# Attention's copies out of PSUM, issued half a slot later, on one core of Trainium2

## The chip, the core and the metric

The kernel runs on one core of one Trainium2 chip. A core has a matrix engine (TensorE, PE in the profile, with its weight loads shown apart as PEld), a vector engine (VectorE, DVE), an activation engine (ScalarE, ACT), GpSimd (POOL) and a queue that issues DMAs (SyncE, SP). Each engine has its own stream of instructions, and semaphores tie the streams together. The metric is the device time of one launch in microseconds (us), the median of several runs; lower is better.

## What is computed

The input x is 4 x 32 x 96 x 256 (batch, variables, segments, channels). Layer 0 normalizes it by groups of channels and sends it through two selective-scan blocks (Mamba), one along the segments and one along the variables. Layer 1 takes the 3072 tokens of each batch, normalizes them, adds attention and then a mixture of four experts, whose gate comes from a graph attention over about a million edges. The part that matters here is the attention, an additive one in which every pair of tokens passes a tanh over 32 units:

```python
def _L1_attn_ref(inputs, Wt, Wx, bh, Wa, ba):
    q = jnp.einsum('bld,du->blu', inputs, Wt)
    k = jnp.einsum('bld,du->blu', inputs, Wx)
    h = jnp.tanh(q[:, :, None, :] + k[:, None, :, :] + bh)
    e = jnp.einsum('biju,u->bij', h, Wa[:, 0]) + ba[0]
    a = jax.nn.softmax(e, axis=-1)
    v = jnp.einsum('bij,bjd->bid', a, inputs)
    return v
...
    x = x + _L0_conv_ref(_gn(x), ...)
    t = _to_tokens(x)
    t = t + _L1_attn_ref(_ln_t(t), L1_attn_Wt, L1_attn_Wx, L1_attn_bh, L1_attn_Wa, L1_attn_ba)
    t = t + _L1_ffn_ref(_ln_t(t), ...)
```

## The kernel before

**Two streams of work, interleaved by hand.** The order of PE, ACT, DVE and POOL is exactly the order in which the program issues instructions; no scheduler moves them. In `whole`, one generator, `att.units`, issues attention, and at each of its `yield`s another one, `steps`, issues a piece of the other work: first layer 0 (`Layer0.run`), then the sorting of edges and a part of the experts. One step of `units` is a *slot*. A slot has two halves:

- attention issues one `th` (L802: a tanh over 128 x 3072 on ACT, for 4 query tokens and 32 units); then comes the first half of the other work;
- attention issues the scores of the `th` of two slots ago (L778, on PE, into the tile `pe`); then comes the second half of the other work;
- at the end of the slot attention does one small *step* from the list `todo`, or a piece of side work (`beside`: keys of the next batch, or the normalized tokens and gate features after attention).

There are 3072 slots of attention and 3072 of layer 0; attention begins when layer 0 has finished the first of the four batches, and so runs beside layer 0 for three batches and beside edges and experts for the fourth.

**Layer 0 in a slot.** Its scans come in a cycle of three slots. In the first half of slot 0 of the cycle there are decays alone (L378: two exponentials on ACT into two PSUM tiles `dA`), in slot 1 two scans of the earlier decays (L395, DVE) and then two decays into the same two tiles, and in slot 2 two scans. The second half has the products that the scans read (dB, L386, DVE), the products with C on POOL (L402), and the parts of the next block's front (convolution, step sizes) and of the last block's end. A decay can be written only when the scan that reads its tile has finished.

**A unit of attention.** Eight slots make the scores of 32 query tokens. In the eighth, `unit_tail` issues the row maximum (nb, L848, DVE) behind the scores, and `weights` the exponential (pr, L855, ACT) at the end of the slot. The steps of the following slots are: four transposes of pr into PSUM (ptw, L862) with their copy to pT (L864, DVE); two more with their copy; the 24 products with the values (pv, L871); the copy of pv to pvs (`kept`, L877). After every fourth unit `tile_tail` follows: `factors` (maxima mx, their transpose pm, the largest of them g, g4), `factors2` (a transpose pf and the differences f), `factors3` (exponential of f, ACT), `spread` (sf, POOL), `together` (products po) and `outputs` (reciprocal, sum with x, statistics, store). When a new unit ends, whatever is left in `todo` is issued at once; in every fourth unit these are `together` and `outputs`.

**Buffers.** All of ptw, pv, pm, pf, po and the PSUM tiles of the side work come from `self.psum`, a pool with a single buffer of one bank (`PV_BUFS` is 1), so a product can begin only when the copy out of the one before has been done. There are three `th` buffers and one `pe`.

**Copies behind their products.** Each step issues its products and, right behind them, the copy out of PSUM that reads them. `us` on a step tells the other stream how much PE time the step will take, and only the early experts, in the fourth batch, use it.

Of the kernel before, what the change touches and what calls it, by code (L numbers as in the profile page):

```python
# [22 lines left out]
ALU = mybir.AluOpType  # L23
AX = mybir.AxisListType
PSUM = bass.MemoryType.PSUM

P = 128
# [15 lines left out]
QU = 32  # L43
NQT = P // QU
# [587 lines left out]
class Attention:  # L632
# [4 lines left out]
    def __init__(self, ctx, tc, ident, a, x1, x2, xn2T, tab_s, tab_a):  # L637
# [33 lines left out]
                                for k, n in (("krep", TOK), ("qsel", TOK // R_ATT)))  # L671
        self.extra, self.entry, self.col, self.asked, self.normed = 0.0, 0, 0, 0, 0

    def psum(self, name):
        return self.ps_v.tile([P, JB], F32, tag="pv", name=name)

# [89 lines left out]
    def units(self, side):  # L766


        nc = self.nc
        todo, behind = [], []  # L770
        NK = QU // R_ATT
        PER = TOK // R_ATT

        def scores(pe, k, th):
            for j in range(2):
                for q in range(NQT):
                    c0 = q * KQ + j * KQ // 2
                    nc.tensor.matmul(pe[q * QU:(q + 1) * QU, j, :KQ // 2], self.wa[:, k, :],  # L778
                                     th[:, c0:c0 + KQ // 2], start=(k == 0), stop=(k == NK - 1))

        def beside():
            while side:
                try:
                    return next(side[0])
                except StopIteration:
                    side.pop(0)

        i = 0  # L790
        while i < B * PER + LAG or todo:
            b, col = self.entry, self.col = divmod(i, PER)
            if b < B and "krep" not in self.state[b]:

                yield
                yield
                beside()
                continue
            if b < B:
                s = self.state[b]  # L800
                th = self.th.tile([P, TOK], F32, tag="th", name="th")
                nc.scalar.activation(th, s["krep"], AF.Tanh, bias=s["qsel"][:, col:col + 1])  # L802
                behind.append(th)
            yield
            busy = tail = None
            if behind and i >= LAG:
                n, k = divmod(i - LAG, NK)
                if k == 0:
                    pe = self.ps_e.tile([P, 2, JB], F32, tag="pe", name="pe")
                scores(pe, k, behind.pop(0))  # L810
                if k == NK - 1:
                    tail = self.unit_tail(*divmod(n, TOK // QU), pe)
                    busy = True

            self.extra = 0.0 if tail or not todo else getattr(todo[0], "us", 0.0)
            yield
            if tail:

                for f in todo:
                    f()  # L820
                todo = tail()
            elif todo:
                busy = todo.pop(0)()

            if b < B and col == LAG + 3:
                self.load_values(b)
            if b < B and LAG + 4 <= col < LAG + 10:
                self.normalize_values(b, col - LAG - 4)
            if b and col == LAG + 10:
                side.append(self.after(b - 1, *AFTER[-1]))  # L830
            side += [self.after(b, t0, t1) for t0, t1 in AFTER[:-1]
                     if b < B and col == t1 * P // R_ATT + LAG + 10]
            if busy is None:
                beside()
            i += 1
        side.append(self.after(B - 1, *AFTER[-1]))

    def unit_tail(self, b, n, pe):

        nc, s = self.nc, self.state[b]  # L840
        NU = P // QU
        t, u = n // NU, n % NU
        if u == 0:
            s["nb"] = self.wk.tile([P, NU], F32, tag="nb", name="nb", bufs=3)
            s["pvs"] = self.wk.tile([P, NU, C + 1], F32, tag="pvs", name="pvs")
        nb, pvs = s["nb"], s["pvs"]
        pes = pe[:, :, :KQ // 2]
        nc.vector.tensor_reduce(nb[:, u:u + 1], pes, AX.XY, ALU.max, negate=True)  # L848
        NK = KQ // P
        v = {}  # L850

        def weights():
            pr = v["pr"] = self.wk.tile([P, KQ], F32, tag="pr", name="pr")
            v["pT"] = self.wk.tile([P, NK, P], F32, tag="pT", name="pT")
            nc.scalar.activation(pr.rearrange("p (j x) -> p j x", j=2), pes, AF.Exp,  # L855
                                 bias=nb[:, u:u + 1])
            return steps

        def turn(i0, i1):
            pt, pr, pT = self.psum("ptw"), v["pr"], v["pT"]  # L860
            for i in range(i0, i1):
                nc.tensor.transpose(pt[:, (i - i0) * P:(i - i0 + 1) * P], pr[:, i * P:(i + 1) * P],  # L862
                                    self.ident)
            nc.vector.tensor_copy(pT[:, i0:i1, :].rearrange("p i x -> p (i x)"),  # L864
                                  pt[:, :(i1 - i0) * P])

        def values():
            pv, pT = self.psum("pv"), v["pT"]
            for i in range(NK):
                for q in range(NQT):  # L870
                    nc.tensor.matmul(pv[q * QU:(q + 1) * QU, :C + 1], pT[:, i, q * QU:(q + 1) * QU],  # L871
                                     s["xn"][:, q * NK + i, :], start=(i == 0), stop=(i == NK - 1))
            s["pv"] = pv
            return "pv"

        def kept():
            nc.vector.tensor_copy(pvs[:, u, :], s["pv"][:, :C + 1])  # L877

        first, second = (lambda: turn(0, 4)), (lambda: turn(4, NK))
        first.us, second.us, values.us = 0.7, 0.4, 2.9  # L880
        steps = [first, second, values, kept]
        if u == NU - 1:
            first, *rest = self.tile_tail(b, t, nb, pvs)
            steps = steps[:3] + [lambda: (kept(), first())[1]] + rest
        return weights

    def tile_tail(self, b, t, nb, pvs):

        nc, s = self.nc, self.state[b]
        NU = P // QU  # L890
        mx = self.wk.tile([P, NU], F32, tag="mx", name="mx", bufs=2)
        sf = self.wk.tile([P, NU, QU], F32, tag="sf", name="sf")
        f = self.wk.tile([P, NU], F32, tag="f", name="f", bufs=2)
        x = self.wk.tile([P, C], F32, tag="x", name="x", bufs=2)
        row0 = b * TOK + t * P
        src = self.x1[b].rearrange("v s c -> (v s) c")[t * P:(t + 1) * P, :]

        def factors():
            nc.sync.dma_start(x, src)
            nc.vector.tensor_scalar(mx, nb, -1.0, self.ba, ALU.mult, ALU.add)  # L900
            g = self.wk.tile([NU, QU], F32, tag="g", name="g")
            g4 = self.wk.tile([NU, NQT, QU], F32, tag="g4", name="g4")
            pm = self.psum("pm")
            nc.tensor.transpose(pm[:NU, :P], mx, self.ident)
            nc.vector.tensor_reduce(g, pm[:NU, :P].rearrange("p (q r) -> p r q", q=NQT), AX.X,
                                    ALU.max)
            nc.vector.tensor_copy(g4, g.unsqueeze(1).to_broadcast([NU, NQT, QU]))
            s["g4"] = g4

        def factors2():  # L910
            pf = self.psum("pf")
            nc.tensor.transpose(pf[:, :NU], s["g4"].rearrange("p q r -> p (q r)"),
                                self.ident[:NU, :NU])
            nc.vector.tensor_tensor(f, mx, pf[:, :NU], ALU.subtract)

        def factors3():
            nc.scalar.activation(f, f, AF.Exp)  # L917

        def spread():
            for u in range(NU):  # L920
                nc.gpsimd.tensor_scalar(sf[:, u, :], self.sel, f[:, u:u + 1], None, ALU.mult)  # L921

        def together():
            po = self.psum("po")
            for u in range(NU):
                nc.tensor.matmul(po[u * QU:(u + 1) * QU, :C + 1], sf[:, u, :], pvs[:, u, :],
                                 start=True, stop=True)
            s["po"] = po
            return "po"

        def outputs():
            po = s["po"]
            sm = self.wk.tile([P, 1], F32, tag="sm", name="sm", bufs=2)
            nc.vector.reciprocal(sm, po[:, C:C + 1])
            nc.vector.scalar_tensor_tensor(x, po[:, :C], sm, x, ALU.mult, ALU.add)
            self.statistics(s["mv2"], t, x)
            nc.sync.dma_start(self.x2[row0:row0 + P, :], x)

        return [factors, factors2, factors3, spread, together, outputs]

    def after(self, b, t0=0, t1=NT):

# [1088 lines left out]
```

## Time and profile before

| | |
|---|---|
| time, median of 3 runs | 15854.98 us (15839.43 to 15862.44) |
| profiled execution | 15480.32 us, its span 15478.4 us |
| PE busy | 11840.1 us, 76% of the span |
| DVE busy | 11076.9 us, 72% |
| ACT busy | 12181.5 us, 79% |
| POOL busy | 8984.7 us, 58% |
| granted PE clock, mean | 0.881 |
| th (L802), ACT | 3072 of 2847 ns, 8665.9 us |
| scans (L395), DVE | 4096 of 940 ns, 3682.6 us |
| copies pT (L864), DVE | 768 of 555 ns, 426.1 us |
| copies pvs (L877), DVE | 384 of 420 ns, 161.2 us |

The profiled execution is 2.4% shorter than the median of the timed runs. The span falls into stages: layer 0 alone up to about 2400 us; layer 0 beside attention from 2700 to 11550, with two short stretches (about 5400 to 5800 and 8500 to 8900) in which attention waits for the keys of the next batch; attention beside the sorting of edges from 11550 to 12750; attention beside the counting of edges by one-hot products up to about 14360; and then the experts and the graph. A share of busy time is a mean over all of these, so the profile has to be read stage by stage. A wait is idle time of the engine that waits; it counts for the end only if that engine is the one that sets it.

### The profile page before, as it was taken

To read this page: it belongs to the slowest core of one execution; us is meant where nothing else is said; L and a number is where in the kernel's file an instruction comes from. 1 tells how busy PE (TensorE), PEld (TensorE's weight loads), DVE (VectorE), ACT (ScalarE), POOL (GpSimd) and SP (SyncE) were. 2 spreads that over 40 slices of the span, in tenths; PEclk is the share of its full clock that TensorE was granted. 3 is DMA by queue.
4 is the path that set the end of the run, shared out by engine and by line. 5 is a ranking of instruction groups with operands and counts; after the bars stand their busy time and mean duration, and the time that the engine had idled before them with its cause. 6 is when DMAs were issued, how large, how long until landed. Compare 5 with 4: busy or idle time off the path is not lost.

```text
span 15478.4 us, 224265 instructions
## 1 busy us (share of the span) xinstructions
PE 11840.1 (76%) x86496; PEld 5192.8 (34%) x86496; DVE 11076.9 (72%) x15711; ACT 12181.5 (79%) x9326; POOL 8984.7 (58%) x6586
## 2 busy tenths in 40 slices
PE   5666665777777777878888777888877878887897
PEld 2222222222222233333333333333333334443454
DVE  7888888777777887777777877577767783331368
ACT  3443334999999979999999899999998989998221
POOL 4565557777777767777777677577750000007663
PEclk8888886888888878889998888999988989998998
DMA  5666665444444444454444444355541000001224
GB/s 190 203 206 200 199 201 163 144 146 152 148 147 148 153 157 145 148 151 149 149 146 154 149 147 150 113 153 153 150 129 40 25 15 15 8 25 22 52 62 127
DMA packets 1197834, 1986.89 MB, mean 128 GB/s; under 512 B 411985, under 2 KB 645073, under 8 KB 1194321
## 3 DMA queue, kind: packets, MB, share of 16 engines
q1 hardware_dynamic: 1169104, 1967.10, 41.1%
q0 software_dynamic: 27648, 5.36, 0.9%
q8 instruction: 680, 11.14, 0.3%
q14 instruction: 402, 3.29, 0.1%
HBM read 1864.71 MB, written 107.35 MB: 127 GB/s over the span
## 4 chain that ended last, share of the span: by engine, by line
ACT 32%; PE 23%; DVE 19%; POOL 11%; issue 10%; DMA 4%; SPq 0%; DVEq 0%; POOLq 0%; ACTq 0%
ACT th L802 23%; PE pe L778 9%; DVE h L395 7%; POOL h L402 5%; ACT dA L378 5%; POOL gd L1009 3%; PE pv L871 2%; DVE dB L386 2%; DMA bB<-bc 2%; PE pa L1333 2%; PE po L1585 1%; ACT pr L855 1%; PE ph L1577 1%; PE ptw L862 1%; POOL uab L312 1%
## 5 line engine op out<-in xcount | busy, mean ns | idle before, releaser
L802 ACT ACTIVATE th<-krep,qsel 128x3072 f32<-128x3072 f32 x3072 | 8665.9, 2847 | 406.0 <-PE pe L778 389.2
L778 PE MATMUL pe<-th,wa_blk 128*32 128x384 f32 x49152 | 5108.5, 544 | 1634.9 <-ACT pr L855 1259.7
L402 POOL TENSOR_TENSOR h<-h,bC 128x768 f32<-128x768 f32 x2048 | 3782.9, 1847 | 2869.2 <-DVE h L395 2641.1
L395 DVE TENSOR_TENSOR_SCAN h<-dA,dB 128x384 f32<-128x384 f32 x4096 | 3682.6, 940 | 822.9 <-ACT dA L378 624.8
L778 PEld LDWEIGHTS pe<-th,wa_blk 128*32 128x32 f32 x49152 | 1470.4, 117 | 4272.4 <-issue 1946.2
L386 DVE TENSOR_TENSOR dB<-bB,dtu 128x768 f32<-128x768 f32 x2048 | 1946.0, 950 | 133.3 <-DMA bB<-bc 89.3
L378 ACT ACTIVATE dA<-dt,t_A 128x380 f32<-128x380 f32 x2048 | 1134.1, 572 | 991.1 <-DVE h L395 985.9
L378 ACT ACTIVATE dA<-dt,d_A 128x372 f32<-128x372 f32 x2048 | 1109.2, 563 | 672.4 <-DVE h L395 666.2
L421 PE MATMUL py<-h,ident 128*128 128x384 f32 x2176 | 992.4, 588 | 688.9 <-POOL h L402 687.7
L921 POOL TENSOR_SCALAR sf<-sel,f 128x32 f32<-128x32 f32 x384 | 153.2, 422 | 2321.1 <-ACT f L917 2321.0
L409 POOL TENSOR_TENSOR h<-h 128x768 f32<-128x768 f32 x752 | 1424.2, 1894 | 46.9
L864 DVE COPY pT<-ptw 128x512 f32<-128x512 f32 (+1 forms) x768 | 426.1, 555 | 1123.9 <-PE ptw L862 1123.0
L871 PE MATMUL pv<-xn,pT 128*32 128x257 f32 x18432 | 1095.2, 385 | 84.2 <-DVE pT L864 82.5
L421 PEld LDWEIGHTS py<-h,ident 128*128 128x128 f32 x2176 | 437.1, 219 | 1248.7 <-POOL h L402 1021.7
L410 POOL TENSOR_TENSOR h<-h 128x384 f32<-128x384 f32 x752 | 798.1, 1061 | 59.0
L411 POOL TENSOR_TENSOR y<-y,h 128x384 f32<-128x384 f32 x752 | 768.3, 1022 | 59.0
L871 PEld LDWEIGHTS pv<-xn,pT 128*32 128x32 f32 x18432 | 586.1, 111 | 634.0 <-DVE pT L864 146.6
L1286 POOL DMA_INDIRECT gs<-tab_s,si x432 | 504.7, 1168 | 265.2 <-issue 121.8
L316 DVE SCALAR_TENSOR_TENSOR uab<-uab 128x384 f32<-128x384 f32 x256 | 389.8, 1523 | 198.6 <-POOL uab L312 194.6
L1659 ACT ACTIVATE h<-ph,b 128x512 f32<-128x512 f32 x148 | 100.4, 687 | 533.3 <-PE ph L1577 533.1
L1009 POOL DMA_INDIRECT gd<-tab_a,di x432 | 428.3, 991 | 133.0 <-issue 133.0
L848 DVE TENSOR_REDUCE nb<-pe 128x1 f32<-128x768 f32 x384 | 362.1, 943 | 197.2 <-PE pe L778 197.0
(292 smaller groups left out, 15388.4 us busy)
## 6 DMA issues: line engine op xcount, KB each, us to landing
bB<-bc SPq DMA_DIRECT2D x2048, 384.0 KB
bC<-bc SPq DMA_DIRECT2D x2048, 384.0 KB
all<-kept SPq DMA_DIRECT2D x19, 2048.0 KB
x<-x SPq DMA_DIRECT2D x144, 256.0 KB
x<-x SPq DMA_DIRECT2D x192, 128.0 KB
xt<-xn2T SPq DMA_DIRECT2D x41, 512.0 KB
kept<-ko SPq DMA_DIRECT2D x39, 512.0 KB
qsel<-xn2T SPq DMA_DIRECT2D x75, 256.0 KB
```

The source lines that it names most:

```text
L378: nc.scalar.activation(inner(dA[:, :T]), inner(blk["dt"][:, e, :]), AF.Exp, scale=blk["w"]["A"][:, e, i + s:i + s + 1])
L386: nc.vector.tensor_tensor(dB, blk["bB"].pop(j), z["dtu"].unsqueeze(1).to_broadcast([P, SB, T]), ALU.mult)
L395: nc.vector.tensor_tensor_scan(h[:, s, :], z.pop(("dA", e, i + s))[:, :T], z["dB"][:, s, :], 0.0, ALU.mult, ALU.add)
L402: nc.gpsimd.tensor_tensor(h, h, blk["bC"].pop(j), ALU.mult)
L409: nc.gpsimd.tensor_tensor(h0, h0, h1, ALU.add)
L410: nc.gpsimd.tensor_tensor(h0[:, 0, :], h0[:, 0, :], h0[:, 1, :], ALU.add)
L411: nc.gpsimd.tensor_tensor(y[e], y[e], h0[:, 0, :], ALU.add)
L421: nc.tensor.matmul(z["py"], self.ident, h[:, s, :], start=(i == 0), stop=(i == DS - 1))
L778: nc.tensor.matmul(pe[q * QU:(q + 1) * QU, j, :KQ // 2], self.wa[:, k, :], th[:, c0:c0 + KQ // 2], start=(k == 0), stop=(k == NK - 1))
L802: nc.scalar.activation(th, s["krep"], AF.Tanh, bias=s["qsel"][:, col:col + 1])
L871: nc.tensor.matmul(pv[q * QU:(q + 1) * QU, :C + 1], pT[:, i, q * QU:(q + 1) * QU], s["xn"][:, q * NK + i, :], start=(i == 0), stop=(i == N ...
L1009: self.nc.gpsimd.indirect_dma_start(out=self.gd[:, q, c, :], out_offset=None, in_=self.tab_a[q].rearrange("p n f -> (p n) f"), in_offset=b ...
```

## The change

The copies out of PSUM (and the other DVE work that reads a product of attention) are no longer issued right behind their products at the end of a slot. They are put on a list, `self.later`, and issued in the next slot between the first half of the other work and the scores, that is, behind layer 0's scans and decays of that slot and in front of its second half. `kept` is no longer a step of its own: pv's copy goes on the list too, and so is issued half a slot earlier than before. The maxima mx and the load of x are issued with the last of these copies, half a slot before the transpose that reads mx. `outputs` comes one slot behind `together`. Side work is issued before the transposes of a step instead of behind them, never in the slot of the value products (`full`), and at as many places as before. Three steps of the tile's tail now have a `us`.

```diff
--- before.py
+++ after.py
@@ -671,6 +671,8 @@
                                 for k, n in (("krep", TOK), ("qsel", TOK // R_ATT)))
         self.extra, self.entry, self.col, self.asked, self.normed = 0.0, 0, 0, 0, 0
 
+        self.later = []
+
     def psum(self, name):
         return self.ps_v.tile([P, JB], F32, tag="pv", name=name)
 
@@ -788,11 +790,14 @@
 
 
         i = 0
-        while i < B * PER + LAG or todo:
+        while i < B * PER + LAG or todo or self.later:
             b, col = self.entry, self.col = divmod(i, PER)
             if b < B and "krep" not in self.state[b]:
 
                 yield
+                late, self.later = self.later, []
+                for f in late:
+                    f()
                 yield
                 beside()
                 continue
@@ -802,6 +807,9 @@
                 nc.scalar.activation(th, s["krep"], AF.Tanh, bias=s["qsel"][:, col:col + 1])
                 behind.append(th)
             yield
+            late, self.later = self.later, []
+            for f in late:
+                f()
             busy = tail = None
             if behind and i >= LAG:
                 n, k = divmod(i - LAG, NK)
@@ -819,8 +827,13 @@
                 for f in todo:
                     f()
                 todo = tail()
+            elif todo and hasattr(todo[0], "us"):
+                if not todo[0].full:
+                    beside()
+                todo.pop(0)()
+                busy = True
             elif todo:
-                busy = todo.pop(0)()
+                todo.pop(0)()
 
             if b < B and col == LAG + 3:
                 self.load_values(b)
@@ -861,8 +874,8 @@
             for i in range(i0, i1):
                 nc.tensor.transpose(pt[:, (i - i0) * P:(i - i0 + 1) * P], pr[:, i * P:(i + 1) * P],
                                     self.ident)
-            nc.vector.tensor_copy(pT[:, i0:i1, :].rearrange("p i x -> p (i x)"),
-                                  pt[:, :(i1 - i0) * P])
+            self.later.append(lambda: nc.vector.tensor_copy(
+                pT[:, i0:i1, :].rearrange("p i x -> p (i x)"), pt[:, :(i1 - i0) * P]))
 
         def values():
             pv, pT = self.psum("pv"), v["pT"]
@@ -870,19 +883,22 @@
                 for q in range(NQT):
                     nc.tensor.matmul(pv[q * QU:(q + 1) * QU, :C + 1], pT[:, i, q * QU:(q + 1) * QU],
                                      s["xn"][:, q * NK + i, :], start=(i == 0), stop=(i == NK - 1))
-            s["pv"] = pv
-            return "pv"
-
-        def kept():
-            nc.vector.tensor_copy(pvs[:, u, :], s["pv"][:, :C + 1])
-
-        first, second = (lambda: turn(0, 4)), (lambda: turn(4, NK))
-        first.us, second.us, values.us = 0.7, 0.4, 2.9
-        steps = [first, second, values, kept]
+            self.later.append(lambda: nc.vector.tensor_copy(pvs[:, u, :], pv[:, :C + 1]))
+
+        steps = [self.step(lambda: turn(0, 4), 0.7), self.step(lambda: turn(4, NK), 0.4),
+                 self.step(values, 2.9, True)]
         if u == NU - 1:
             first, *rest = self.tile_tail(b, t, nb, pvs)
-            steps = steps[:3] + [lambda: (kept(), first())[1]] + rest
+            steps[2] = self.step(lambda: (values(), self.later.append(first)), 2.9, True)
+            steps += rest
         return weights
+
+    @staticmethod
+    def step(f, us, full=False):
+
+        g = lambda: f()
+        g.us, g.full = us, full
+        return g
 
     def tile_tail(self, b, t, nb, pvs):
 
@@ -895,23 +911,29 @@
         row0 = b * TOK + t * P
         src = self.x1[b].rearrange("v s c -> (v s) c")[t * P:(t + 1) * P, :]
 
-        def factors():
+        def maxima():
             nc.sync.dma_start(x, src)
             nc.vector.tensor_scalar(mx, nb, -1.0, self.ba, ALU.mult, ALU.add)
+
+        def factors():
             g = self.wk.tile([NU, QU], F32, tag="g", name="g")
             g4 = self.wk.tile([NU, NQT, QU], F32, tag="g4", name="g4")
             pm = self.psum("pm")
             nc.tensor.transpose(pm[:NU, :P], mx, self.ident)
-            nc.vector.tensor_reduce(g, pm[:NU, :P].rearrange("p (q r) -> p r q", q=NQT), AX.X,
-                                    ALU.max)
-            nc.vector.tensor_copy(g4, g.unsqueeze(1).to_broadcast([NU, NQT, QU]))
             s["g4"] = g4
+
+            def late():
+                nc.vector.tensor_reduce(g, pm[:NU, :P].rearrange("p (q r) -> p r q", q=NQT), AX.X,
+                                        ALU.max)
+                nc.vector.tensor_copy(g4, g.unsqueeze(1).to_broadcast([NU, NQT, QU]))
+
+            self.later.append(late)
 
         def factors2():
             pf = self.psum("pf")
             nc.tensor.transpose(pf[:, :NU], s["g4"].rearrange("p q r -> p (q r)"),
                                 self.ident[:NU, :NU])
-            nc.vector.tensor_tensor(f, mx, pf[:, :NU], ALU.subtract)
+            self.later.append(lambda: nc.vector.tensor_tensor(f, mx, pf[:, :NU], ALU.subtract))
 
         def factors3():
             nc.scalar.activation(f, f, AF.Exp)
@@ -925,18 +947,17 @@
             for u in range(NU):
                 nc.tensor.matmul(po[u * QU:(u + 1) * QU, :C + 1], sf[:, u, :], pvs[:, u, :],
                                  start=True, stop=True)
-            s["po"] = po
-            return "po"
-
-        def outputs():
-            po = s["po"]
+            self.later.append(lambda: outputs(po))
+
+        def outputs(po):
             sm = self.wk.tile([P, 1], F32, tag="sm", name="sm", bufs=2)
             nc.vector.reciprocal(sm, po[:, C:C + 1])
             nc.vector.scalar_tensor_tensor(x, po[:, :C], sm, x, ALU.mult, ALU.add)
             self.statistics(s["mv2"], t, x)
             nc.sync.dma_start(self.x2[row0:row0 + P, :], x)
 
-        return [factors, factors2, factors3, spread, together, outputs]
+        return [maxima, self.step(factors, 0.2), self.step(factors2, 0.1), factors3, spread,
+                self.step(together, 1.5, True)]
 
     def after(self, b, t0=0, t1=NT):
 
```

## The prediction

> **What bounds the kernel now.** I read the page's slices first, then the busy time by stretch, then ACT's waits stretch by stretch, then the group of the copy, and last a piece of timeline. In the slices (tenths of busy time in 40 equal parts of the span) ACT stands at 9 from slice 7 to slice 36 with a few dips; before and after that it is not the limit.
>
> ```profile
> PE   5666665777777777878888777888877878887897
> DVE  7888888777777887777777877577767783331368
> ACT  3443334999999979999999899999998989998221
> ```
>
> Cut into stretches, the columns are window, length, then busy time (and count) of PE, PE's weight loads, DVE, ACT, POOL, then clock and DMA.
>
> ```profile
> 2700.00:5400.00 2700.00, 2016.13 (x17219) 757.85 (x17216) 2087.85 (x2698) 2615.06 (x1969) 2075.90 (x1482) 0.87 0.48 148
> 5800.00:8500.00 2700.00, 2184.98 (x17508) 943.16 (x17509) 2032.93 (x2771) 2552.71 (x1903) 1969.97 (x1410) 0.90 0.49 149
> 8900.00:11550.00 2650.00, 2145.35 (x17646) 913.92 (x17645) 1904.03 (x2643) 2532.40 (x1838) 1847.95 (x1329) 0.90 0.48 144
> 11550.00:12750.00 1200.00, 922.45 (x8543) 389.39 (x8543) 930.46 (x1499) 1023.87 (x422) 27.71 (x41) 0.90 0.09 28
> 12750.00:14000.00 1250.00, 1100.26 (x11704) 519.10 (x11703) 454.70 (x876) 1211.89 (x497) 84.94 (x121) 0.93 0.06 17
> ```
>
> The first three (layer 0 beside attention; I call them mixed) leave ACT 84.9, 147.3 and 117.6 us idle, the sorting stretch 176.1, the one-hot stretch 38.1. That is 564 us, and no reordering of DVE can bring more than this from these stretches. What ACT waits for, in the second mixed stretch (first two lines) and in the sorting stretch (last two; us, times, longest):
>
> ```profile
> ACT dA L378 <- DVE h L395: 76.8, 118, 3.6
> ACT th L802 <- PE pe L778: 61.9, 62, 3.9
> ...
> ACT th L802 <- PE pe L778: 116.1, 92, 8.0
> ACT pr L855 <- DVE nb L848: 70.1, 19, 14.2
> ```
>
> So the end is set by ACT, and ACT is held by a late scan on DVE or by late scores on PE. The copy that the change is about is DVE's largest idle group:
>
> ```profile
> L864 DVE COPY pT<-ptw 128x512 f32<-128x512 f32 (+1 forms) x768 | 426.1, 555 | 1123.9 <-PE ptw L862 1123.0
> ```
>
> 1123 us is idle time of DVE, not of ACT. How one turns into the other is seen in one unit of the first mixed stretch:
>
> ```profile
> 3911.07 1.06 ACT L378 ACTIVATE dA<-dt,d_A 128x372 f32<-128x372 f32 x2
> ...
> 3914.04 0.62 PE L862 MATMUL ptw<-ident,pr 128*128 128x128 f32 x4
> ...
> 3914.69 0.69 DVE L864 COPY pT<-ptw 128x512 f32<-128x512 f32 x1 [4.69 <-PE ptw L862]
> 3915.30 1.80 DVE L395 TENSOR_TENSOR_SCAN h<-dA,dB 128x384 f32<-128x384 f32 x2
> ...
> 3923.56 0.57 ACT L378 ACTIVATE dA<-dt,d_A 128x372 f32<-128x372 f32 x1 [0.80 <-DVE h L395]
> ```
>
> DVE stood 4.69 us at the copy; the scans behind it had their decays at 3912.13 and began at 3915.30, 3.2 us late; 8 us on, ACT waited 0.80 us for a scan. Most of the loss was made up on the way: 4.69 us on DVE cost ACT about 1 us.
>
> [...] Attention has one bank for all these products (PV_BUFS = 1), so the next product waits for the copy: the trace has PE waiting 82.5 us for pT at the value products. [...]
>
> **The change part by part.** All engines keep the same instructions (DVE 16,486, PE 49,916 in the two streams put side by side), so nothing is added or removed; only order differs, and almost only on DVE. ACT's and POOL's orders are the same but for a few dozen places (ACT 58 lines of difference, 13 of them table loads that move, none more), so no ACT time comes or goes. SP's loads of x are issued half a slot earlier, and its other differences are neighbours swapped; no transfer is on ACT's path here, cost nothing.
>
> (a) *pT copies behind the next slot's scans.* 508 of the 768 move. The other third falls in slots whose first half gives DVE nothing (only decays), and there the order is as it was. In the moved ones the scans no longer wait for PE. ACT's waits for scans are 55.6 + 76.8 + 34.9 = 167.3 us in the mixed stretches. Bounds: 0 and -167. I take 60%, -100 us: two thirds of the copies move, and part of these waits stands behind other DVE work (conv taps, statistics).
>
> (b) *Tile tail.* mx is now computed in front of the half slot that transposes it. PE waited for it 39.5 + 24.4 + 8.5 = 72.4 us in the mixed stretches; DVE's waits for pm, pf and po (g 10.3 + 36.2 + 29.8, f and sm less) go too. PE's lateness costs ACT through th: 22.5 + 61.9 + 64.1 = 148.5 us. A quarter of the 72: -20 us (bounds 0, -50).
>
> (c) *What is now late: the value products.* Second copy pT comes behind the scans, and the 24 value products (2.8 us of PE) cannot start before it; everything behind them on PE, the next scores first, is late too, and ACT's Tanh, with three th buffers, waits for these. I went through the timeline unit by unit, put both copies behind what they now pass (scans at the earliest after their decays), and noted how much later the value products start, and how much time the Tanh that needs the following scores had to spare. Mean delay 0.77, 1.05, 0.77 us in the three mixed stretches; mean spare time 2.17, 1.17, 1.28. Units whose delay exceeds their spare time lose 8 + 34 + 20 = 62 us. Bounds 0 and 220 (all delay counts: 90 x 0.77 + 82 x 1.05 + 84 x 0.77). I take +45, since DVE will also reach these places earlier.
>
> (d) *pvs copy half a slot earlier.* It waited little as a step of its own (17.3, 8.5, 21.5 us). It now meets the value products while they run; in front of dB in a third of the slots. DVE has slack there (75 to 77% busy) and dB is needed only about 4 us later (a Tanh of 2.85 and two decays of 0.57): 0, bounds 0 and +40.
>
> (e) *Sorting stretch.* DVE there is full: 930 busy and 138 waiting at pT of 1200. Freed of that wait, it comes to nb earlier; ACT's 70.1 us for nb lose some 50. Against it both copies now stand behind one or two sort operations of 1.2 us: value products 1.80 us later in the mean over 43 units, spare time 0.51, loss 57. Net 0, bounds -120 and +60.
>
> (f) *One-hot stretch* (ACT 97% busy, DVE's 308 us of waiting at pT cover nothing ACT needs): 0, bounds -30 and +45. The two pauses of attention for keys (5400 to 5800, 8500 to 8900) run hardly any steps: 0. The end of attention, where DVE waited 79.8 us at sm: -10.
>
> (g) *The side work before the transposes instead of after.* One wait for the single bank either way: 0, bounds -20 and +20.
>
> Sum: -100 - 20 + 45 + 0 + 0 - 10 = -85 us on the profiled execution of 15480.3 us. The timed runs have a median of 15855, 1.024 times that, so about -87: **15768 us**.
>
> **Rivals.** *Balanced* (no change): ACT's waits for scans go, and the same time appears as th waiting for scores, since the value products start later. For it: 62 us is a low count if delays add up from unit to unit. Against it: PE's large wait for pr (345.6, 254.6, 243.5 us) resets PE once a unit. About 15855.
>
> *The value products decide* (slower): one mechanism, copies behind scans or sort operations keep PE from starting values, and PE reaches the next scores after ACT has used up its th buffers. It decides from the point where the mean delay exceeds the spare time, 1.2 to 2.2 us in the mixed stretches; in the sorting stretch it already does. Price: all of 62 + 57 + 45 = 164 us, with the gains of (a), (b) halved (-60) and no gain at nb: about +104, 15960 us. For it: PE is 81% busy in the second and third stretch, and one bank chains copy to product. Against it: first copies are hardly late (0.13 to 0.34 us).
>
> *The sorting stretch opens* (much faster): nb and pr lose their waits, th follows, ACT goes from 1024 of 1200 to near full: -120 there, (a) at -140: about 15600.
>
> **How the numbers follow.** What a measurement of this kernel can tell from no change is about 0.2%, 32 us. Forecast 0.43, sorting opens 0.15, balanced 0.16, value products 0.26. Nearly all of the first two lies beyond -32 us: faster 0.57. Balanced is within 0.2% in most of its cases: same 0.14. The rest, slower 0.29. The likeliest's own range is 15680 to 15840 ((a) between -60 and -150, (c) between 0 and +90); for 8 in 10 the range reaches 15610 on the side of the open sorting stretch and 15945 on that of the value products.
>
> **What would show it.** In the profile after: DVE's wait at pT for ptw well under half of 1123 us, and ACT's dA waiting for h in the three mixed stretches near 70 instead of 167: step (a). PE's wait for mx near nothing: (b). PE's wait for pT at the value products well above 82.5 us, and th waiting for pe somewhat up: (c). If th's waits in the mixed stretches rise by over 100 us, or the sorting stretch gets longer, the prediction is wrong on the side of the second rival; if the sorting stretch gets shorter by 100 us, on that of the third.

## The result, and the profile after

| | before | after |
|---|---|---|
| time, median of 8 runs each | 15853.51 us (15839.43 to 15873.08) | 15799.44 us (15785.0 to 15823.88) |
| ratio, 95% interval | 1 | 0.9966 [0.9955, 0.9976] |
| mean time by the ratio's interval | | 38 to 71 us less |

The change makes the kernel 54 us faster: the sign and the range of the prediction hold, its 87 us are 1.6 times too many. The slices of the page after, to be set against those of before (tenths of busy time in 40 equal parts):

```profile
PE   5666665777777777878887787888768788845797
DVE  7888888778777887777777876677777843301367
ACT  3443336999999989999998999999979999945121
```

ACT is still the full engine from slice 7 on. The new 4 and 5 near the end of its row are not the change's doing; they are taken up at the end of this section. The same five stretches as before, with the same columns:

```profile
2700.00:5400.00 2700.00, 2029.55 (x17479) 768.55 (x17472) 2116.40 (x2762) 2638.39 (x1986) 2102.83 (x1496) 0.88 0.48 151
5800.00:8500.00 2700.00, 2171.30 (x17570) 939.95 (x17562) 2012.46 (x2803) 2549.96 (x1901) 1970.23 (x1403) 0.91 0.48 149
8900.00:11550.00 2650.00, 2120.74 (x17609) 906.94 (x17605) 1908.34 (x2665) 2519.88 (x1819) 1807.51 (x1299) 0.91 0.46 142
11550.00:12750.00 1200.00, 954.72 (x8996) 404.43 (x8988) 930.30 (x1521) 1059.33 (x438) 24.57 (x45) 0.92 0.09 27
12750.00:14000.00 1250.00, 1030.46 (x10838) 472.72 (x10834) 408.71 (x777) 1121.06 (x457) 92.71 (x126) 0.90 0.05 15
```

ACT (fourth busy time) gains 23 us of work in the first mixed stretch and 35 in the sorting stretch; in the second and third it loses 3 and 13. So of the three mixed stretches only the first became better. The copies' groups say why DVE looks so much better all the same (out<-in, count | busy, mean ns | idle before, its largest releaser):

```profile
L877 DVE COPY pT<-ptw 128x512 f32<-128x512 f32 (+1 forms) x768 | 417.2, 543 | 760.0 <-PE ptw L875 538.9
L886 DVE COPY pvs<-pv 128x257 f32<-128x257 f32 x384 | 161.0, 419 | 786.8 <-PE pv L884 688.0
```

DVE's wait for the transposes falls from 1123.0 to 538.9 us, and a wait for the value products, 244.8 us in all before (336.9 in the second profile of before, see below), grows to 688.0. Engine waits in the second mixed stretch (first four lines) and in the sorting stretch (last three):

```profile
DVE pvs L886 <- PE pv L884: 117.3, 63, 3.4
PE pv L884 <- DVE pT L877: 86.9, 35, 5.9
ACT th L807 <- PE pe L780: 80.3, 69, 3.8
ACT dA L378 <- DVE h L395: 52.7, 99, 4.0
...
ACT th L807 <- PE pe L780: 102.2, 86, 6.7
DVE pT L877 <- PE ptw L875: 61.8, 26, 10.4
ACT pr L868 <- DVE nb L861: 32.6, 16, 7.6
```

In the mixed stretch ACT waits 24.1 us less for scans and 18.4 more for scores: three quarters of the gain are handed back, and PE's wait for pT went from 15.1 to 86.9 us. That the later scores come from this wait is tested below.

For differences of a few microseconds I cut every profile where attention begins (the first `th`) and at its `th` number 768, 1536, 2304, 2610 and 2880, which are the starts of the batches and, roughly, the end of sorting and of the one-hot products (batch 2 as cut here ends at 11848 us in before, some 300 us after layer 0). The kernel before was profiled a second time, beside the experiments, as a control:

> The kernel before, unchanged, for a second profile. All profiles since show about 340 us more in the stretch of attention in which the edges are gathered (about 13680 to 14670 us) than the first profile of before, whose span of 15478 us lies 375 us under the timed median. If the pause belongs to the kernel as timed, this run is at 15850 us with the stretch at about 990 us; if it comes with the changed order, the run is at 15480 us with 654 us there.

It took 15838.49 us. Its stages against those of the first profile and of after (us):

| stage | before, first | before, again | after | after less before again |
|---|---|---|---|---|
| layer 0 alone | 2568.3 | 2547.9 | 2554.7 | +6.8 |
| batch 0 beside layer 0 | 3076.1 | 3076.1 | 3039.6 | -36.5 |
| batch 1 beside layer 0 | 3170.8 | 3169.6 | 3164.7 | -4.9 |
| batch 2 beside layer 0 | 3033.0 | 3034.1 | 3039.0 | +4.9 |
| sorting | 1035.5 | 1035.5 | 1002.1 | -33.4 |
| one-hot | 815.1 | 811.5 | 813.0 | +1.5 |
| gathers | 653.6 | 988.1 | 994.0 | +5.9 |
| rest | 1126.0 | 1173.7 | 1186.1 | +12.4 |

The two profiles of before agree within 1.2 us in the three batches and in sorting, so there a difference of several us means something, though of after and of every kernel below there is one profile. The change brings 36.5 us in batch 0, nothing in batches 1 and 2 together, and 33.4 us in sorting. The gather stage is 334 us longer in the second profile of before as well, so this stretch (the 4 and 5 in ACT's slices) is no effect of the change. It also adds to DVE's wait for the value products: 80.8 us in that stage in the first profile, 172.8 in the second.

### The profile page after: what moved, and what is told of

Same layout as the page of the kernel before. It is cut to its first block, busy times and chain, and to the rows that moved or that the text cites. A ratio compares the mean times of both kernels' runs of the same rounds, so it can differ in the third digit from the quotient of the medians.

```text
span 15793.1 us, 224204 instructions
## 1 busy us (share of the span) xinstructions
PE 11831.0 (75%) x86496; PEld 5165.5 (33%) x86496; DVE 11047.2 (70%) x15711; ACT 12179.4 (77%) x9326; POOL 8986.7 (57%) x6586
## 4 chain that ended last, share of the span: by engine, by line
PE 21%; ACT 17%; DVE 8%; issue 6%; POOL 2%; another core or an unknown queue 1%; DMA 1%; SPq 0%; DVEq 0%; ACTq 0%; POOLq 0%
ACT th L807 12%; PE pe L780 8%; PE pv L884 4%; ACT dA L378 2%; PE pa L1354 2%; DVE h L395 2%; PE ph L1598 2%; PE po L1606 2%; ACT pr L868 1%; POOL h L402 1%; PE ptw L875 1%; PE ex L1523 1%; PE px L215 1%; DVE dB L386 1%
## 5 line engine op out<-in xcount | busy, mean ns | idle before, releaser
L780 PE MATMUL pe<-th,wa_blk 128*32 128x384 f32 x49152 | 5053.7, 539 | 1526.9 <-ACT pr L868 1249.4
L884 PE MATMUL pv<-xn,pT 128*32 128x257 f32 x18432 | 1190.7, 400 | 473.1 <-issue 281.1
L877 DVE COPY pT<-ptw 128x512 f32<-128x512 f32 (+1 forms) x768 | 417.2, 543 | 760.0 <-PE ptw L875 538.9
L886 DVE COPY pvs<-pv 128x257 f32<-128x257 f32 x384 | 161.0, 419 | 786.8 <-PE pv L884 688.0
L875 PE MATMUL ptw<-ident,pr 128*128 128x128 f32 x2304 | 477.4, 325 | 178.3 <-DVE pT L877 69.3
L875 PEld LDWEIGHTS ptw<-ident,pr 128*128 128x128 f32 x2304 | 304.6, 164 | 661.4 <-issue 320.2
```

## The experiments

The edits are against the changed kernel, except for `side_only`. In the runs a row of switches makes them; the diffs below write out what the switches come to, and are shortened. Times are set against runs of before on the same chip. In the texts written ahead, the letters name the theories as each text gives them.

**Which of pT's two moves pays.** Before, the two copies share a line, but by form they differ:

```profile
L864 DVE COPY pT<-ptw 128x512 f32<-128x512 f32 x384 | 264.9, 690 | 918.1 <-PE ptw L862 917.9
L864 DVE COPY pT<-ptw 128x256 f32<-128x256 f32 x384 | 161.1, 420 | 205.8 <-PE ptw L862 205.1
```

The first copy (four transposes) waited 2.39 us each time (917.9 / 384), the second (two) 0.53 us. The second has little to give, and the value products start only behind it. `second_now` puts the second copy back behind its transposes:

```diff
-            self.later.append(copy)
+            if i0 == 0:
+                self.later.append(copy)
+            else:
+                copy()
```

> The changed kernel, but the second pT copy of a unit (two transposes) is again issued right behind its products; all else as changed. Theory A (the gain is the scans freed of the first copy, the loss is value products that start late behind the second copy): the first copy had 918 of the 1123 us of waiting before, so nearly all of the gain stays, and PE's wait for pT at the value products falls from 190 us to about 85, ACT's th waits for scores in the three layer-0 stretches fall by about 45 us: 15740 to 15775 us, faster than the changed kernel's 15799. Theory B (the freed scans are the whole effect and late value products cost nothing): part of the gain is given back, 15805 to 15830 us.

15750.2 us, ratio 0.9936 [0.9922, 0.9949]: 97 us faster than before, 49 faster than after, as theory A has it. `pT_now` puts both back (`copy()` alone):

> The changed kernel, but both pT copies are again issued right behind their products; the copy of pv, the tile tail's reads of PSUM and the side work in front of the transposes stay as changed. Theory A: without the scans freed, ACT's dA waits for h return to about 300 us in the three layer-0 stretches (from 205), th waits fall by some 30: 15840 to 15870 us. Theory C (the gain is the tile tail and the earlier pv copy, pT's place doesn't matter): the time stays at 15790 to 15810 us.

15799.48 us, 0.9971 [0.9959, 0.9983]: the time of after, where theory C has it; A, which gave all of the gain to pT, missed. So moving the first copy brings 49 us (55 by the ratios). Moving the second costs 49 by the medians, 48 by the ratios, and 43 if each kernel is set against its own runs of before. The two together bring about nothing, and the 48 us by which `pT_now` is faster than before come from the rest of the change. The first copy's move is shown once more by `side_only` and `first_side` below, which differ in it alone: 15836.8 and 15797.89 us on the same chip, 39 us, with intervals that do not overlap. The waits of the two kernels in the second mixed stretch, `second_now` first:

```profile
ACT th L808 <- PE pe L781: 59.2, 59, 2.8
ACT dA L379 <- DVE h L396: 50.9, 108, 3.6
PE pv L887 <- DVE pT L880: 10.5, 5, 4.0
```

```profile
ACT dA L379 <- DVE h L396: 63.8, 123, 3.6
ACT th L808 <- PE pe L781: 56.6, 58, 2.8
PE pv L887 <- DVE pT L880: 13.5, 12, 4.5
```

With the first copy late, the wait for scans falls from 63.8 to 50.9 us and PE's wait for pT does not rise. With the second late too (after, above), scans do not get earlier (52.7), PE waits 86.9 us, and `th` 80.3 instead of 59.2. The stretches of fixed time leave out the edges of the batches, so here are the same waits over batches 0 to 2 as a whole (before is its second profile):

| us | before | after | second_now | pT_now |
|---|---|---|---|---|
| ACT dA waits for h | 302.5 | 203.4 | 219.1 | 262.8 |
| ACT th waits for pe | 214.4 | 259.5 | 205.5 | 194.4 |
| all idle time of ACT | 583.5 | 551.4 | 507.9 | 544.1 |
| idle time, against before | | -32.1 | -75.6 | -39.4 |
| length of the batches, against before | | -36.5 | -77.0 | -35.7 |
| PE pv waits for pT | 70.5 | 177.8 | 17.8 | 48.4 |

ACT's idle time follows the length of the batches within 5 us in all three kernels, so these rows carry the account: the second copy's move buys 16 us of scans and pays 54 of scores; the first copy's buys 44 of scans and pays 11 of scores. One cost of the change appears in neither row: ACT's exponential of f now waits for DVE, 29.7 us over these batches in after, 0 in before and in `tail_now` below.

**How the late copy costs.** One unit of batch 1 in the timeline of after (start, duration, what, count, idle before and its end):

```profile
6612.44 0.44 PE L875 MATMUL ptw<-ident,pr 128*128 128x128 f32 x2
...
6613.18 1.70 DVE L160 TENSOR_SCALAR d_xproj<-d_xproj 128x64 f32<-128x64 f32 x1
6613.91 2.85 ACT L807 ACTIVATE th<-krep,qsel 128x3072 f32<-128x3072 f32 x1
6616.67 1.06 ACT L378 ACTIVATE dA<-dt,t_A 128x380 f32<-128x380 f32 x2
6617.27 1.80 DVE L395 TENSOR_TENSOR_SCAN h<-dA,dB 128x384 f32<-128x384 f32 x2 [2.39 <-ACT dA L378]
...
6618.99 0.40 DVE L877 COPY pT<-ptw 128x256 f32<-128x256 f32 x1
...
6619.44 5.37 PE L884 MATMUL pv<-xn,pT 128*32 128x257 f32 x48 [5.13 <-DVE pT L877]
...
6626.46 2.87 ACT L807 ACTIVATE th<-krep,qsel 128x3072 f32<-128x3072 f32 x1 [2.19 <-PE pe L780]
```

The transposes were done at 6612.88. DVE was free at 6614.88, but the scans at the head of its queue wanted decays that ACT, with a `th` of 2.85 us in front of them, gave at 6617. DVE stood 2.39 us in front of scans that were not ready, with a ready copy behind them: the fault of the kernel before, the other way round. PE stood 5.13 us, and 7.5 us after the copy ACT waited 2.19 us for scores.

The value products themselves took 5.37 us here. In the same unit of `second_now`:

```profile
6620.42 0.44 PE L878 MATMUL ptw<-ident,pr 128*128 128x128 f32 x2
...
6623.38 0.41 DVE L880 COPY pT<-ptw 128x256 f32<-128x256 f32 x1
6623.84 2.82 PE L887 MATMUL pv<-xn,pT 128*32 128x257 f32 x48 [1.55 <-DVE pT L880]
```

2.82 us for the same 48 instructions (two for each of the 24 products) after 1.55 us of idle. The granted clock was 0.50 in the 5.37 us of after. In batch 1 of after, the 64 units whose values began after less than 0.5 us of idle took 2.83 us in the mean, 14 that began after 1.24 to 1.62 us took 2.82 each at a granted clock of 1.00, and the 14 that began after 3.73 to 5.95 us took 4.84 in the mean at 0.50 to 0.67. The length of that one wait is not all, though: six units of batch 0 of after took 4.4 to 4.5 us, at 0.62 to 0.63, after waits of 1.0 to 2.3. In batch 1 of `second_now` PE waits for pT at the values 5 times, 10.5 us in all, against 39 times and 91.6 us in after. In batch 1 of before three units began after 3.95 to 5.17 us, and the value products of that batch took 277.4 us against 299.4 in after. In those 14 units the late copy thus cost PE 2.0 us in the mean (4.84 less 2.83) beyond the wait itself.

Why batch 1 and not batch 0? A unit has 8 slots and layer 0's block 48, so a unit's steps meet the block at six fixed positions. In batch 1 of after, 70 of the 91 us that PE waits for pT fall to one of the six (16 units, 4.4 us each), the one shown; in batch 0 the largest is 22 us. The six stand differently to the scans in batch 0 than in batches 1 and 2. That the position decides is read from the traces; no run shifted it.

**The experts.** Batches 1 and 2 also have early experts on PE. The next pair does no expert work beside layer 0 (the same work is done later, so only the stages of batches 1 and 2 are compared), with both pT copies late and with only the first:

```diff
-        self.jobs = [(b, e, j) for b in range(B - 2) for e in range(NEXP) for j in range(n)]
+        self.jobs = []
```

> The changed kernel with no experts beside layer 0 (their work is done later, in the early experts and the tail; the time as a whole is longer and is not compared). Only the stages of the second and third batch count, against the next run. Theory A with PE's load: with experts gone, PE has time to spare, and a late second copy costs nothing or gains, as in the first batch: these two stages are not longer than those of the next run. Theory B' (the experts are not the reason): they stay about 25 us longer each.

> The pair to the run before: no experts beside layer 0, second pT copy right behind its products. Theory A with PE's load: second and third batch as long as, or some 10 us longer than, those of the run before. Theory B': about 25 us shorter each.

Batch 1 takes 3035.0 and 3015.4 us, batch 2 2926.4 and 2911.1. The late second copy still costs 19.6 and 15.3 us; with experts it was 24.7 and 27.7 (3164.7 less 3140.0, 3039.0 less 3011.3). Theory A with PE's load is refuted, and B' is near. By these single profiles PE's load by experts is the smaller part of the cost, about a fifth in batch 1 and under half in batch 2.

**The copy of pv.** `pv_step` makes it a step of its own at the end of the next slot again. In every fourth unit the maxima mx go back with it, right in front of their transpose, so two moves are undone at once:

```diff
-            self.later.append(lambda: nc.vector.tensor_copy(pvs[:, u, :], pv[:, :C + 1]))
+            v["kept"] = lambda: nc.vector.tensor_copy(pvs[:, u, :], pv[:, :C + 1])
...
+        steps.append(lambda: v["kept"]())
```

> The changed kernel, but the copy of pv is again a step of its own at the end of the slot after the value products, half a slot later than in the changed kernel; pT copies and tile tail stay as changed. DVE's wait for pv rose from 245 to 688 us with the change. Theory A as predicted (that wait is covered by the time until dB is needed): nothing on ACT, 15790 to 15810 us. Theory D (DVE standing at pv in front of dB eats a part of the gain, since dA still waits 205 us for h): 15750 to 15780 us.

15781.53 us, 0.9961 [0.9947, 0.9974]: 18 us less than after by the medians, 8 by the ratios, whose intervals overlap widely, so a gain is not shown. Batch 0 is 17 us longer and batch 1, batch 2 and sorting are 10, 8 and 9 shorter. PE's wait for mx over batches 0 to 2 is back at 70.3 us (17.7 in after, 85.2 in before), so what pv's copy does alone stays open. `first_pv` has this edit and that of `second_now` together:

> The changed kernel with the second pT copy right behind its products and pv's copy a step of its own at the end of the next slot; first pT copy, tile tail and side order as changed. If the two gains found alone (49 and 18 us against the changed kernel) add up: 15725 to 15745 us. If pv's place costs only where values are late (theory A, then one gain contains the other): 15745 to 15760 us.

15774.06 us, 0.9943 [0.993, 0.9957]: above both ranges, and no better than `second_now` alone (0.9936, intervals overlap). The two gains do not add up. As mx goes back here too (PE waits 89.1 us for it), this doesn't show whether pv's copy is better early or late.

**The tile's tail.** `tail_now` issues g, g4, f and the outputs right behind their products:

```diff
-            self.later.append(late)
+            late()
...
-            self.later.append(lambda: nc.vector.tensor_tensor(f, mx, pf[:, :NU], ALU.subtract))
+            nc.vector.tensor_tensor(f, mx, pf[:, :NU], ALU.subtract)
...
-            self.later.append(lambda: outputs(po))
+            outputs(po)
```

> The changed kernel, but the tile tail's reads of PSUM (g, g4, f and the outputs) are again issued right behind their products; mx stays half a slot earlier, pT and pv copies as changed. Theory A: 20 to 30 us of the gain are given back, in the three layer-0 stretches and at attention's end (DVE's waits for pm, pf, po return, about 270 us in all): 15815 to 15835 us. Theory C (the tail is the gain): all of it is given back, about 15850 us.

15790.81 us, 0.9963 [0.9949, 0.9976], not distinguishable from after, and both theories missed: beside a late second copy this move shows no gain. mx stays early here. `first_side` is `first_pv` with the tail at once:

> As the run before it, but the tile tail's reads of PSUM right behind their products as well: what stays of the change is the first pT copy behind the scans and the side order. The tail made no difference alone (15791 against 15799): 15735 to 15765 us if that holds here too; if tail and second copy are tied through the single bank, 15770 to 15800 us.

15797.89 us, 0.9958 [0.9944, 0.9972], 24 us above `first_pv` by the medians (batch 1 +9, batch 2 +13, sorting +20). The two intervals overlap, but all five runs of one lie above all five of the other, on the same chip. With the values early, the late tail does seem to bring what after does not show; why is not shown.

**The side work alone.** `side_only` has before's order of copies, with the side work in front of the transposes:

> The kernel before with one part of the change alone: the side work (keys, gate features) is issued in front of the two transposes of a step instead of behind them; every copy out of PSUM, pv's step and the tile tail stay as before. The four runs so far left 15800 us with both pT copies back in place, so about 50 us of gain come from something else than pT. Theory E (it is the order of the side work): 15790 to 15810 us. Theory C (it is pv's copy, mx and the tail together): 15840 to 15860 us, as the kernel before.

15836.8 us, 0.9987 [0.998, 0.9994] over 18 runs: about 20 us (10 to 32 by the interval), between the two theories. It is a part of the 48 that `pT_now` keeps, not all of them; the other 28 or so, a difference between two chips, belong to the tail, the early mx and the copy of pv, which no run separated with pT's copies in this place.

**A version that joins the two.** Batch 0 liked the second copy late (3039.6 us in after, 3051.5 in `second_now`), so `second_first_batch` keeps it late there only:

```diff
-            self.later.append(copy)
+            if i0 == 0 or b == 0:
+                self.later.append(copy)
+            else:
+                copy()
```

> The changed kernel with the second pT copy late only in the first batch of attention and right behind its products in the other three. By the stages of the profiles, the late second copy gained 12 us in the first batch (3040 against 3052 us, no experts beside it) and cost 25 and 28 us in the second and third (experts beside, PE 80% busy). If that is PE's load, the stages add up: about 12 us under the run with the second copy at once everywhere, 15730 to 15745 us. If the difference between batches was scatter: 15745 to 15760 us.

15341.05 us against 15461.94 for before, 0.9926 [0.9912, 0.9939]: 121 us. Batch 0 takes 3036.5 us, batches 1 and 2 3137.8 and 3011.8, like the better of the two kernels in each, so the stages add up, though by the runs without experts PE's load is not the main reason. Against `second_now` the gain is 0.1%, inside both intervals, so that the whole kernel is faster than `second_now` is not shown. This run, the pair without experts and the next one fell on a chip on which before itself is 392 us shorter, which is why the absolute times expected do not fit.

**The pause at the gathers.** `sparse_gather` is `second_first_batch` with one indirect gather per slot instead of three; what remains is gathered after attention:

```diff
-        for _ in range(3 if columns else 0):
+        for _ in range(1 if columns else 0):
```

> As the run before it, but in the last stretch of attention one gather of the edges' table is issued a slot instead of three (what is not gathered there is gathered in the tail, nothing is left out). If the pause of some 340 us, which the second profile of before shows as well, comes from gathers issued back to back on POOL, that stretch falls from about 990 to under 850 us, and the tail takes back part of it: 15550 to 15720 us. If it does not come from the gathers, the stretch stays and the tail gets longer: 15740 to 15850 us.

15427.67 us, 0.9978 [0.9969, 0.9988]: the gather stage takes 593.9 us instead of 646.6, the rest 1274.3 instead of 1128.7. As this chip shows no pause with three gathers either, the run does not answer what it was made for.

## Why the prediction came out as it did

- **(a) pT behind the scans, -100: the term that was wrong.** It took both copies as one, from a row that joins two forms, and priced them by the number that move. In its own stretches ACT's waits for scans fell by 65 us (167.3 to 102.2), not 100, and only 34 of these belong to the first copy (148.0 in `pT_now`, 114.0 in `second_now`), 12 to the second and 19 to the rest of the change. Over whole batches they fell by 99 us, of which 44 and 16 belong to the two copies. In device time the first copy's move is worth 39 to 49 us, sorting included; the second's buys fewer scans than it pays scores.
- **(b) Tile tail, -20, and (g) side work, 0.** PE's wait for mx fell from 72.4 to 17.0 us as foreseen. By the runs the two steps, with the copy of pv, make 48 us. The side work alone is about 20 instead of 0, so (g) was too small. What is left for (b) and pv, some 28, is near the 20 of (b), but no run gives mx alone, and the late f brings ACT a wait of its own that the term left out.
- **(c) Values late, +45: right in mechanism, and in size as a sum.** The mean delay foreseen was 0.77, 1.05 and 0.77 us; PE's wait for pT rose by 0.02, 0.88 and 0.45 us a unit (1.7, 71.8 and 37.5 us over 90, 82 and 84 units). ACT's waits for scores rose by 36.9 us in these stretches (148.5 to 185.4), and taking the second copy's move back saves 43 to 49. That the sum came out is in part luck: the delay was smaller than foreseen and its price higher, and the lower clock of the values after a long wait (0.50 in the 5.37 us above) was not in the step. The 82.5 us that the prediction set beside the single bank are waits for a copy whose result, pT, the products read, and not for the bank alone; no run gave attention a second bank.
- **(d) Copy of pv, 0.** DVE's wait there grew from 244.8 us (336.9 in the second profile of before) to 688.0; taking it back together with mx brings 8 to 18 us, not clear of the noise and within the bounds.
- **(e) Sorting, 0.** The stage became 33.4 us shorter. ACT's wait for nb fell from 70.1 to 32.6 us, 37 of the 50 foreseen. The 57 us of late values did not come: by stage, PE's wait for pT at the values is 11.6 us before and after. The lateness that the step counted there does not appear as a wait, and ACT's waits for scores in the stage fell too, from 75.2 to 58.3 us.
- **(f) One-hot and the end.** +1.5 us in the one-hot stage: right. The 10 us at the end of attention lie in the gather stage, whose pause covers them. The pauses for keys were not 0: from one `th` to the next 85 us pass in the first and 13 in the second, not 400. In the two stretches ACT's waits for scans fell from 128.8 to 93.9 us, and those for scores rose from 20.5 to 29.2.
- **The scale 1.024** from profile to timed runs was no scale but added time behind the change: 334 us in the gather stage and 48 in the rest. On a change of 85 us this made 2.

Sum: the mixed stages gave 36.5 us instead of the 75 of (a) to (d), and sorting 33.4 instead of 0. That the total lies inside the range is in part luck, since these two misses cancel. Of the prediction's own signs, PE's waits for mx and for pT came as said; DVE's wait at pT fell to 48%, not well under half, and ACT's waits for scans to 102 us, not to about 70. The stages that the change hardly touches (layer 0 alone, gathers, the rest) are 25 us longer in the one pair of profiles; layer 0 alone differs by 20 between two profiles of before, and the rest is not explained. Of the rivals, *balanced* was half right: for the pair of pT's moves it is what happened as a whole (15799.48 us without them, 15799.44 with them). By stages the pair gains 29 us in batch 0 and 17 in sorting and loses 10 and 19 in batches 1 and 2. *The value products decide* had the mechanism of that loss, but not its size.

## What to carry to other kernels

Before copies are moved as a group, split their row by form and ask of each copy two things: how long the engine waited at it, and who waits for it. A copy that waits long and is needed late is the one to move behind other work (here a gain of 39 to 49 us); the last copy in front of a long product is the one to leave in place (a loss of 43 to 49 us here, though batch 0 alone gained 12), above all if the work that it would stand behind waits for yet another engine (2.39 us in the unit shown). And PE, kept waiting for 3.73 to 5.95 us, ran the value products here at a granted clock of 0.50 to 0.67 (4.84 us in the mean instead of 2.83), so a delay cost more than its length. Test such moves singly: a switch that moves two things, as `pv_step` moved mx along, leaves open which of them counted.

## What the runs showed that was not expected

**A pause at the gathers, in some profiles.** In the gather stage attention runs beside indirect DMAs that POOL issues one behind the other. In the second profile of before, PE, its weight loads and ACT there:

```profile
13961.32 0.94 POOL L1009 DMA_INDIRECT gd<-tab_a,di  x1 [0.30 <-issue]
13962.00 0.59 PE L871 MATMUL pv<-xn,pT 128*32 128x257 f32 x1 [2.21 <-issue]
13962.56 0.94 POOL L1009 DMA_INDIRECT gd<-tab_a,di  x1 [0.30 <-issue]
13963.40 0.13 PEld L871 LDWEIGHTS pv<-xn,pT 128*32 128x32 f32 x1 [2.67 <-issue]
...
13969.07 2.85 ACT L802 ACTIVATE th<-krep,qsel 128x3072 f32<-128x3072 f32 x1 [51.76 <-remote]
```

"issue" is idle time for which the profile shows no wait. PE executes single instructions 2 to 3 us apart, and ACT waits 51.76 us for its next `th`. The stage lasts 988.1 us; in the first profile of before, and in the three runs of the last chip with three gathers per slot, it lasts 647 to 656, with the same 324 gathers of 0.95 us in it. The time of before was 15854 us on one chip and 15462 on the other, so most of the difference is this stretch. Its cause stays open: the gathers run beside it, but they do so where there is no pause too, and the run with fewer of them met no pause to take away.

**Slower value products after an idle stretch.** The same 48 value instructions took 2.82 us at a granted clock of 1.00 and 5.37 at 0.50. Of 96 units of batch 1, 14 in after began after 3.73 to 5.95 us of idle and ran at 0.50 to 0.67, three in before after 3.95 to 5.17 us, at 0.50 to 0.62.
